# One exponential and one logarithm for the first image's preparation, the last halves' routing after the last weights, and roots by GpSimd's power

## The chip, the cores and the metric

The kernel runs on one core of a Trainium2 chip. The metric is device time in microseconds, the median of several executions. The core has five engines with instruction queues of their own: TensorE (PE) for matmuls, VectorE (DVE), ScalarE (ACT), GpSimd (POOL) and SyncE (SP), which issues transfers here. An engine takes its instructions in order, so one that waits holds up all those behind it.

## The reference

The input `x` is 4 images of 256 channels and 32 x 32 places, so 1024 tokens an image. Two layers follow one another; cut to what matters:

```python
# layer 0
x = x + proj(attention(ln_c(x)) + pe)         # 8 heads, softmax over the dyn_k highest scores of a row
t = tokens(x)
t = t + moe0(ln_t(t))                         # 8 experts, the best 2, 256 -> 256 -> 256, exact GELU; moe0(u) = u + experts
x = image(t)
# layer 1
u = ln_c(x)
delta = softplus(u @ W_delta + b_delta)
Bm, Cm = u @ W_B, u @ W_C
h[l] = exp(delta[l] * -exp(A_log)) * h[l-1] + delta[l] * u[l] * Bm[l]     # 16 states
y = sum over states of h * Cm, + u * D        # in four orders of the places, and their mean
x = x + y
t = tokens(x)
t = t + moe1(ln_t(t))                         # 8 experts, the best 2, 256 -> 1024 -> 256
```

`ln_c` and `ln_t` subtract the mean over channels and divide by the root of the variance plus 1e-6 or 1e-5.

## The kernel before, in words

**Stages.** Norms and projections run to about 110 us, the attention to about 1960, the layer-0 expert tiles to about 2196, the scans of layer 1 to about 3432, and the layer-1 expert tiles to the end.

**Attention** is an order of 64 half-head turns (8 heads, 2 halves, 4 images), each of which finds the threshold of 128-row groups by counting and then masks, exponentiates and sums. `turn(i)` writes out the order by hand. At five places in a turn (`PLACES`) it calls `beside`, which takes a step from other work: `plan(first, needed, steps)` puts a generator on the list `todo`, with the place from which it may run and the turn at which it is due, and `beside` takes the one that is due earliest. A generator that yields True goes on at the next call before others do. The last turns carry three of these: `doubts()`, which checks that all thresholds were found (`all_sure` L977 and L978, matmul `tot` L980, `bad` L982), and `last_image(0)` and `last_image(1)`, which route the two halves of the last image.

**Routing of a half** is `halved`. PE multiplies the tokens by the router (`raw`, L356) and transposes them into PSUM (`tp`, called `turned` in the profile, L361). ACT copies each 128 tokens into the rows to be sent (L366) and squares them in place with a sum along the row (L367), which gives the variance. DVE finds the two best experts (L371 to L382), PE counts how many tokens each expert has (`counted`, L225 to L230), DVE takes the root of the variance by a bit trick and three Newton steps (L387 to L393), ACT forms one exponential (L394), and DVE works out places and weights (L398 to L412). POOL then sends the rows to their experts' slots in memory (`send`, L214), and `table` makes the list of tiles.

In these last turns the attention itself ends: PE forms scores (L878) and adds the mask (L883), ACT exponentiates (L891), PE sums with the values (L901), DVE divides (L910, L911), PE projects (L713) and DVE adds the residual (L716).

**Layer-0 expert tiles.** `Tile0` has 256 rows of one expert. SP loads rows and weights, DVE and ACT normalise (`xn`, L1449 and L1451), PE transposes (L1458), DVE copies (`xe`, L1460), PE multiplies (`hp`, L1483), ACT applies GELU (`hid`, L1485), PE multiplies again (`yp`, L1491), DVE adds the bias (`ys`, L1494), ACT and DVE scale and add the residual (L1498, L1500) and POOL stores (L1502). There are 36 such tiles. After each tile the loop takes up to six steps from each generator in a list `beside`: among them, from the tile FIRST − 1 on, gathering image 0's results (`whole(0)`, L1882), its preparation for the scans and then `lead`, and from SECOND − 1 on `whole(1)`. The order of the instructions of this stage within an engine is chosen by the framework's scheduler from priorities, not by hand.

**Preparation**, `Prep.steps`, is a generator too. For one image: mean and difference `xm`, squares `ln_sq`, variance `ln_ve`, its root by the bit trick and three Newton steps on DVE (L1794 to L1798), multiplication (`ln_rb`), the 32 rows of B and C (`bp`, L1815 to L1818, stored to memory as `bc_d`), then four parts `zp` of the projection (L1837). Softplus is built as max(z, 0) + ln(1 + exp(−|z|)): relu (L1841), absolute value (L1842), exponential (L1843), what adding 1 loses of the exponential (`lost`, two DVE operations), logarithm (L1847), and then sums and products (L1851 to L1856). `whole_rows` is False for the first image, whose preparation runs beside the tiles, and True for the others, which are prepared during the scans. Where `whole_rows` is True the parts at the end are whole rows of 1024. In the tile stage `xm` and `ln_sq` share a tag with two buffers, and `bc` and `v` share the buffer `sp`.

**Lead** is the start of the first scan: `lead_cum` (L1920) on DVE, `lead_uu` (L1922) on POOL and a copy of it on ACT.

**Scans.** There are 4 x 2 x 16 turns of one image, one half of the channels and one state, in an order written by hand. In a turn DVE runs the forward scan `forth` (L2055), the backward scan `back` (L2062, into PSUM), the product `yc` (L2089), the short scan `come` over rows (L2068), then a step of the other generators, preparation and routing, and then the column scan `h` (L2079). ACT forms decays (L2022, L2026, L2030) and a column copy of the inputs (L2039); POOL forms `gap` (L2059), the inputs `uu` (L2038) and `da_c` (L2073); PE adds all directions into one sum (L2044, L2050, L2084) and the outputs over the states (L2093).

Of the kernel before, what the change touches and what calls it, by code (L numbers as in the profile page):

```python
# [14 lines left out]
I32 = mybir.dt.int32  # L15
I8 = mybir.dt.int8
AF = mybir.ActivationFunctionType
ALU = mybir.AluOpType
# [5 lines left out]
C = 256  # L24
# [3 lines left out]
NT = L // P  # L28
# [34 lines left out]
def metaformer(ctx: ExitStack, tc: tile.TileContext, t: dict, out: bass.AP):  # L63
    nc = tc.nc
# [279 lines left out]
    def halved(b, h, space, bank, wide_bank):  # L344
# [17 lines left out]
        yield True  # L362
        nc.vector.tensor_scalar(nm, raw[:, :, E], -C ** -0.5, None, ALU.mult)
        nc.vector.tensor_copy(lg, raw[:, :, :E])
        for i in range(M):
            nc.scalar.copy(xr[b][:, M * h + i, :C], tp[:, i])  # L366
            nc.scalar.activation(tp[:, i], tp[:, i], AF.Square, bias=nm[:, i : i + 1], scale=C ** -0.5,  # L367
                                 accum_out=ve[:, i : i + 1])

        def best(value, hot):  # L370
            nc.vector.tensor_reduce(value, lg, AX.X, ALU.max)  # L371
# [98 lines left out]
    with ExitStack() as st:  # L470
# [454 lines left out]
        def plan(first, needed, steps, places=range(PLACES)):  # L925
            todo.append([first, needed, steps, False, places])
# [48 lines left out]
        def doubts():  # L975
            sure = p2.tile([P, 1], F32, tag="fr", name="all_sure", bufs=1)
            nc.vector.tensor_reduce(sure, fine, AX.XY, ALU.add)  # L977
            nc.vector.tensor_scalar(sure, sure, 2.0 * (2 * B * NT) * 4 - 0.5, None, ALU.is_ge)  # L978
            tot = bank("tot")[:, 0:1]
            nc.tensor.matmul(tot, mean_w, sure, start=True, stop=True)  # L980
            yield True
            nc.vector.tensor_scalar(bad, tot[0:1], (P - 0.5) / C, None, ALU.is_lt)  # L982
            yield False

        plan(70 * PLACES, 100.5, doubts())

        def last_image(h):
            while not images[B - 1].ready[h]:
                yield None
            yield from halved(B - 1, h, scratch("space1"), bank, lambda: wide_ps("turned"))  # L990
            if h == NHALF - 1:
                yield from table(scratch("space2"), bank)

        for h in range(NHALF):
            plan((68 + 2 * h) * PLACES, 100 + h, last_image(h))

        def beside(i, place=None):

# [759 lines left out]
    class Prep:  # L1758
# [7 lines left out]
        def steps(self, room, psum, tag, whole_rows):  # L1766
# [4 lines left out]
            for h in range(NHALF):  # L1771
# [6 lines left out]
                    nc.vector.tensor_tensor(xm[:, c, cols], x[b][:, c, cols], mean, ALU.subtract)  # L1778
                    nc.scalar.activation(sq[:, c, cols], xm[:, c, cols], AF.Square)
                yield  # L1780
            ve, r0, rr, rs = (room(f"ln_{i}", [NT]) for i in ("ve", "r0", "rr", "rs"))
            for h in range(NHALF):
                var = psum.tile([P, HALF], F32, tag=tag, name="ln_var")[:, : NT // NHALF]
                for i in range(NT // NHALF):
# [6 lines left out]
                if h == 0:  # L1791
                    yield
            yield
            nc.vector.tensor_scalar(r0.bitcast(I32), ve.bitcast(I32), -0.5, RSQRT_BITS, ALU.mult, ALU.add)  # L1794
            for src, dst in ((r0, rs), (rs, r0), (r0, rs)):
                nc.vector.tensor_tensor(rr, src, src, ALU.mult)
                nc.vector.scalar_tensor_tensor(rr, rr, -0.5, ve, ALU.mult, ALU.mult)
                nc.vector.scalar_tensor_tensor(dst, rr, 1.5, src, ALU.add, ALU.mult)  # L1798
            yield
            yield  # L1800
            for h in range(NHALF):
# [27 lines left out]
            def lost(c, cols):  # L1829
                back = self.dx[:, c, cols]  # L1830
                nc.vector.tensor_scalar(back, v[:, c, cols], 1.0, 1.0, ALU.add, ALU.subtract)
                nc.vector.tensor_tensor(back, v[:, c, cols], back, ALU.subtract)

            for i, (c, cols) in enumerate(parts):
                zp = psum.tile([P, HALF], F32, tag=tag, name="zp")
                for k in range(CT):
                    nc.tensor.matmul(zp, wd[:, k, ts(c, P)], xm[:, k, cols], start=(k == 0), stop=(k == CT - 1))  # L1837
                if i:
                    lost(*parts[i - 1])
                yield  # L1840
                nc.scalar.activation(self.delta[:, c, cols], zp, AF.Relu, bias=bd[:, c : c + 1])  # L1841
                nc.scalar.activation(v[:, c, cols], zp, AF.Abs, bias=bd[:, c : c + 1])  # L1842
                nc.scalar.activation(v[:, c, cols], v[:, c, cols], AF.Exp, scale=-1.0)  # L1843
                yield
            lost(*parts[-1])
            yield
            nc.scalar.activation(v, v, AF.Ln, bias=1.0)  # L1847
            yield
            for c, cols in [(c, slice(0, L)) for c in range(CT)] if whole_rows else parts:
                dx = self.dx[:, c, cols]  # L1850
                nc.vector.tensor_tensor(dx, dx, v[:, c, cols], ALU.add)  # L1851
                nc.vector.tensor_tensor(self.delta[:, c, cols], self.delta[:, c, cols], dx, ALU.add)
                yield
                yield
                nc.vector.tensor_tensor(dx, self.delta[:, c, cols], xm[:, c, cols], ALU.mult)
                nc.vector.scalar_tensor_tensor(x[b][:, c, cols], xm[:, c, cols], dsk[:, c : c + 1],  # L1856
                                               x[b][:, c, cols], ALU.mult, ALU.add)
                yield
                yield
# [69 lines left out]
    with ExitStack() as st:  # L1929
# [4 lines left out]
        def room(name, shape):  # L1934

            tag = "d" if name in ("xm", "ln_sq") else name
            return pb.tile([P, *shape], F32, tag=tag, name=name, bufs=1 if name == "sp" else None)
# [477 lines left out]
```

## Time and profile before

| | us |
|---|---|
| median of three executions | 3968.95 (3959.26, 3968.95, 3977.5) |
| the profiled execution, its span | 3982.76, 3979.8 |
| PE busy | 3387.3 (85%) |
| DVE busy | 3024.2 (76%) |
| ACT busy | 2799.2 (70%) |
| POOL busy | 1934.2 (49%) |
| granted PE clock, whole span | 0.875 |

By stage, from the same execution:

| stretch, us | PE busy | DVE busy | ACT busy | POOL busy | granted PE clock |
|---|---|---|---|---|---|
| 110 to 1960, attention | 1463.85 | 1609.88 | 1635.08 | 1032.32 | 0.78 |
| 1960 to 2196, layer-0 tiles | 190.16 | 161.25 | 112.58 | 91.95 | 0.90 |
| 2196 to 3432, scans | 1132.06 | 1133.68 | 875.48 | 712.47 | 0.97 |
| 3432 to 3960, layer-1 tiles | 498.47 | 78.16 | 141.23 | 90.46 | 0.98 |

A line of a timeline gives the start and the duration in microseconds, the engine, the source line, the operation, the tile written and the tiles read with their shapes, and how many neighbouring instructions are merged in it. Brackets give the engine's idle time just before and what ended it. Busy time is a sum over an engine's instructions; an idle engine costs nothing unless another waits for it.

### The profile page before, as it was taken

How to read it: one execution, taken by the hardware profiler on the slowest of the kernel's cores; microseconds unless marked ns; L12 is line 12 of the kernel's file. 1: busy time of each engine (PE TensorE's matmuls, PEld its weight loads, DVE VectorE, ACT ScalarE, POOL GpSimd, SP SyncE). 2: the span in 40 equal slices, each digit the busy share in tenths (PEclk: the TensorE clock that was granted, in tenths of full speed). 3: DMA queues.
4: the chain of work that ended last, by engine and by line, in shares of the span. 5: the costliest groups of instructions: out<-in, count | busy, mean ns of one | idle time of the engine just before them, and what ended most of it. 6: DMA issues, size and time to landing. Idle time of an engine off the chain costs nothing. (4 is left out here: it accounts for less than half of the span.)

```text
span 3979.8 us, 49680 instructions
## 1 busy us (share of the span) xinstructions
PE 3387.3 (85%) x17330; PEld 1898.6 (48%) x17330; DVE 3024.2 (76%) x5204; ACT 2799.2 (70%) x3748; POOL 1934.2 (49%) x1671
## 2 busy tenths in 40 slices
PE   8477888888888888886597889988988989999996
PEld 5133443534354444543375333443433433788885
DVE  3589898998989898989476899999999999201112
ACT  2889999899989999996245677767767767322222
POOL 0145544585648574685343667555555556221111
PEclk8578887788778787788798999999999999999997
DMA  9400075000000000000284444334324333655555
GB/s 295 106 1 1 1 221 134 1 1 25 17 1 1 1 33 1 1 11 17 95 243 129 130 122 138 116 111 125 125 100 131 123 116 128 214 187 184 187 194 187
DMA packets 241814, 393.71 MB, mean 99 GB/s; under 512 B 31888, under 2 KB 182160, under 8 KB 241424
## 3 DMA queue, kind: packets, MB, share of 16 engines
q1 hardware_dynamic: 218016, 340.54, 27.5%
q0 software_dynamic: 19904, 48.48, 3.8%
q8 instruction: 139, 2.28, 0.2%
q10 hardware_dynamic: 3632, 1.40, 0.1%
q14 instruction: 123, 1.01, 0.1%
HBM read 280.41 MB, written 109.94 MB: 98 GB/s over the span
## 5 line engine op out<-in xcount | busy, mean ns | idle before, releaser
L823 POOL TENSOR_SCALAR dr<-s_n,last 128x1024 bf16<-128x1024 f32 x250 | 719.4, 2893 | 734.3 <-DVE state L851 396.8
L733 ACT ACTIVATE junk_a<-s_n,state 128x1024 int8<-128x1024 f32 x448 | 514.7, 1149 | 25.3 <-DVE state L857 9.0
L2073 POOL TENSOR_TENSOR da_c<-prod,come 128x1024 f32<-128x1024 f32 x128 | 256.6, 2005 | 389.3 <-DVE h L2079 333.7
L737 DVE TENSOR_SCALAR_CACHE_REDUCE junk_v<-s_n,state 128x1024 int8<-128x1024 f32 x320 | 408.7, 1277 | 8.8
L2263 ACT ACTIVATE hid<-hp,b 128x256 f32<-128x256 f32 x288 | 134.1, 474 | 361.6 <-PE hp L2261 361.3
L784 DVE SCALAR_TENSOR_TENSOR w<-s_n,win 128x1024 f32<-128x1024 f32 x256 | 350.9, 1371 | 5.3
L787 DVE MAX8 win<-w 128x8 f32<-128x1024 f32 x256 | 314.5, 1228 | 8.8
L2084 PE MATMUL sum<-h,ident 128*128 128x512 f32 x512 | 261.4, 635 | 61.3 <-DVE h L2079 59.1
L2062 DVE TENSOR_TENSOR_SCAN sum<-da,uu 128x1024 f32<-128x1024 f32 x127 | 289.9, 2282 | 29.7 <-PE sum L2044 22.2
L891 ACT ACTIVATE ex<-sT 128x1024 f32<-128x1024 f32 x256 | 247.0, 1016 | 88.6 <-PE sT L883 88.5
L2038 POOL TENSOR_TENSOR uu<-dx,bb 128x1024 f32<-128x1024 f32 x127 | 308.3, 2428 | 1.6 <-DMA bb<-bc_d 1.6
L733 ACT ACTIVATE junk_a<-s_n,guess 128x1024 int8<-128x1024 f32 x256 | 294.3, 1150 | 7.2
L2055 DVE TENSOR_TENSOR_SCAN h<-da,uu 128x1024 f32<-128x1024 f32 x127 | 288.4, 2271 | 1.1 <-POOL uu L2038 1.1
L2079 DVE TENSOR_TENSOR_SCAN h<-da_c,uu 128x1024 f32<-128x1024 f32 x127 | 288.8, 2274 | 0.0
L901 PE MATMUL o_ps<-ex,vT 128*32 128x256 f32 x2048 | 238.0, 448 | 57.0 <-ACT ex L891 43.6
L2050 PE MATMUL sum<-da_c,ident 128*128 128x512 f32 x512 | 255.8, 623 | 26.0 <-POOL da_c L2073 22.4
L2272 DVE TENSOR_TENSOR ys<-yp,b2e 128x512 f32<-128x512 f32 x36 | 24.9, 691 | 326.3 <-PE yp L2269 326.3
L2022 ACT ACTIVATE da_c<-delta,a_log 128x1024 f32<-128x1024 f32 x128 | 268.4, 2097 | 5.2 <-DMA rows_y<-ys 5.2
L2261 PE MATMUL hp<-xe,w 128*128 128x256 f32 x1152 | 259.2, 383 | 9.4 <-DVE xe L2249 5.9
L2274 POOL DMA_INDIRECT results<-ys,to x72 | 69.3, 962 | 407.3 <-DVE ys L2272 200.3
L2050 PE MATMUL sum<-h,twice 128*128 128x512 f32 x512 | 248.0, 607 | 12.0 <-DVE sum L2062 12.0
L767 ACT COPY s_n<-sp 128x1024 f32<-128x1024 f32 x256 | 245.4, 1003 | 18.1 <-PE sp L759 10.3
(676 smaller groups left out, 7557.4 us busy)
## 6 DMA issues: line engine op xcount, KB each, us to landing
cb<-bc_d SPq DMA_DIRECT2D x128, 512.0 KB, 4.1
bb<-bc_d SPq DMA_DIRECT2D x127, 512.0 KB, 5.0
w<-in_w SPq DMA_DIRECT2D x36, 1024.0 KB, 5.3
w2e<-in_w SPq DMA_DIRECT2D x36, 1024.0 KB, 5.5
slots_x<-zeros SPq DMA_DIRECT2D x1, 33669.0 KB
slots_x<-zeros SPq DMA_DIRECT2D x1, 33282.0 KB
w<-in_w SPq DMA_DIRECT2D x72, 256.0 KB, 3.1
xs<-slots_x SPq DMA_DIRECT2D x36, 261.0 KB, 3.3
```

The costliest lines, as they stand in the source:

```text
L733: nc.scalar.activation(junk, self.row(r), AF.Sign, bias=thr, scale=-1.0, accum_out=u)
L737: nc.vector.tensor_scalar(junk, self.row(r), thr, None, ALU.is_lt, ALU.add, accum_out=u)
L784: nc.vector.scalar_tensor_tensor(w, self.row(r), self.win[:, r, 0:1], self.row(r), ALU.is_gt if r < LAST_DVE else ALU.is_ge, ALU.subtract, ...
L787: nc.vector.max(out=self.win[:, r, 1:], in_=w)
L823: ins = eng.tensor_scalar(dr, self.row(r), self.last[:, r : r + 1], None, ALU.is_lt)
L2022: nc.scalar.activation(grid(self.da_c), cols_flipped(self.prep.delta[:, self.c]), AF.Exp, scale=self.decay)
L2038: nc.gpsimd.tensor_tensor(self.uu[:, 0], self.prep.dx[:, self.c], self.bb, ALU.mult)
L2050: nc.tensor.matmul(self.sum[:, ts(h, HALF)], ident if eye is None else eye, view[:, ts(h, HW // NHALF), :], start=False, stop=last)
L2055: nc.vector.tensor_tensor_scan(rows.rearrange("p r w -> p (r w)"), self.da, self.uu[:, 0], 0.0, ALU.mult, ALU.add)
L2062: nc.vector.tensor_tensor_scan(self.sum[:, ::-1], self.da[:, ::-1], self.uu[:, 0][:, ::-1], 0.0, ALU.mult, ALU.add)
L2079: nc.vector.tensor_tensor_scan(self.hs, self.da_c, self.uu[:, 1], 0.0, ALU.mult, ALU.add)
L2084: nc.tensor.matmul(cols_flipped(self.sum[:, ts(h, HALF)]), ident, grid(self.hs)[:, :, ts(h, half)], start=False, stop=False)
```

## The change

Three things are edited. In `halved`, the squares go to a scratch row and come before the copies. In the plans, `doubts()` comes two turns' worth of places earlier, and the first half's routing three places later. In `Prep.steps`, the root is one operation of GpSimd, for all images; and where `whole_rows` is False, the four exponentials are one over all four parts, followed at once by the logarithm into the buffer `sq`, with the `lost` operations after that.

```diff
@@ halved
+        junk = room([C])
+        for i in range(M):
+            nc.scalar.activation(junk, tp[:, i], AF.Square, bias=nm[:, i : i + 1], scale=C ** -0.5,
+                                 accum_out=ve[:, i : i + 1])
         for i in range(M):
             nc.scalar.copy(xr[b][:, M * h + i, :C], tp[:, i])
-            nc.scalar.activation(tp[:, i], tp[:, i], AF.Square, bias=nm[:, i : i + 1], scale=C ** -0.5,
-                                 accum_out=ve[:, i : i + 1])
@@ the plans
-        plan(70 * PLACES, 100.5, doubts())
+        plan(68 * PLACES, 99.5, doubts())
...
         for h in range(NHALF):
-            plan((68 + 2 * h) * PLACES, 100 + h, last_image(h))
+            plan((68 + 2 * h) * PLACES + 3 * (1 - h), 100 + h, last_image(h))
@@ Prep.steps
-            ve, r0, rr, rs = (room(f"ln_{i}", [NT]) for i in ("ve", "r0", "rr", "rs"))
+            ve, rs = room("ln_ve", [NT]), room("ln_rs", [NT])
...
-            nc.vector.tensor_scalar(r0.bitcast(I32), ve.bitcast(I32), -0.5, RSQRT_BITS, ALU.mult, ALU.add)
-            for src, dst in ((r0, rs), (rs, r0), (r0, rs)):
-                nc.vector.tensor_tensor(rr, src, src, ALU.mult)
-                nc.vector.scalar_tensor_tensor(rr, rr, -0.5, ve, ALU.mult, ALU.mult)
-                nc.vector.scalar_tensor_tensor(dst, rr, 1.5, src, ALU.add, ALU.mult)
+            nc.gpsimd.tensor_tensor(rs, ve, minus_half, ALU.pow)
...
-                if i:
+                if i and whole_rows:
                     lost(*parts[i - 1])
                 yield
                 nc.scalar.activation(self.delta[:, c, cols], zp, AF.Relu, bias=bd[:, c : c + 1])
                 nc.scalar.activation(v[:, c, cols], zp, AF.Abs, bias=bd[:, c : c + 1])
-                nc.scalar.activation(v[:, c, cols], v[:, c, cols], AF.Exp, scale=-1.0)
+                if whole_rows:
+                    nc.scalar.activation(v[:, c, cols], v[:, c, cols], AF.Exp, scale=-1.0)
                 yield
-            lost(*parts[-1])
-            yield
-            nc.scalar.activation(v, v, AF.Ln, bias=1.0)
-            yield
+            log = v if whole_rows else sq
+            if whole_rows:
+                lost(*parts[-1])
+                yield
+                nc.scalar.activation(log, v, AF.Ln, bias=1.0)
+                yield
+            else:
+                nc.scalar.activation(v, v, AF.Exp, scale=-1.0)
+                nc.scalar.activation(log, v, AF.Ln, bias=1.0)
+                yield
+                for part in parts:
+                    lost(*part)
+                    yield
...
-                nc.vector.tensor_tensor(dx, dx, v[:, c, cols], ALU.add)
+                nc.vector.tensor_tensor(dx, dx, log[:, c, cols], ALU.add)
```

`minus_half` is a column of −0.5 that the kernel had already. `lost` is unchanged: dx = v − ((v + 1) − 1).

## The prediction

> **What bounds the kernel.** I read the page first, then the busy time cut by stage, then the timelines of the three places that the diff touches.
>
> ```profile
> PE 3387.3 (85%) x17330; PEld 1898.6 (48%) x17330; DVE 3024.2 (76%) x5204; ACT 2799.2 (70%) x3748; POOL 1934.2 (49%) x1671
> ...
> PE 12%; DMA 1%; issue 1%; POOL 0%; DVE 0%; ACT 0%; DVEq 0%; POOLq 0%; SPq 0%
> ```
>
> The whole span is bound by no one engine, so each edit must be priced in its own stage. The chain that ended last follows only the last stage: all but a few shares are the matmuls of the layer-1 expert tiles, which the change leaves alone.
>
> The second view is busy time by stretch inside the layer-0 expert tiles. Columns are PE, PEld, DVE, ACT, POOL, the granted clock, the DMA share and GB/s.
>
> ```profile
> 1976.00:2080.00 104.00, 95.13 (x449) 76.92 (x447) 77.62 (x270) 46.70 (x97) 51.11 (x60) 0.97 0.80 236
> ...
> 2112.00:2157.00 45.00, 30.72 (x104) 21.15 (x103) 27.09 (x66) 33.34 (x44) 14.49 (x10) 0.83 0.46 126
> ```
>
> In the quiet stretch PE works 95 of 104 us at a clock of 0.97: those tiles are PE's. In 2112 to 2157, where the first image is prepared for the scans, PE works 31 of 45 us at 0.83 and ACT is the busiest. ACT's timeline there (start, duration, line, operation; idle before it in brackets) says why.
>
> ```profile
> 2126.97 1.28 ACT L1843 ACT_TABLE_LOAD   x1
> 2128.27 0.63 ACT L1843 ACTIVATE sp<-sp 128x512 f32<-128x512 f32 x1
> 2128.91 1.28 ACT L1485 ACT_TABLE_LOAD   x1
> 2130.21 0.47 ACT L1485 ACTIVATE hid<-hp,b1e 128x256 f32<-128x256 f32 x1
> ...
> 2136.94 1.28 ACT L1847 ACT_TABLE_LOAD   x1
> 2138.23 1.91 ACT L1847 ACTIVATE sp<-sp 128x2048 f32<-128x2048 f32 x1
> ```
>
> Every exponential of the preparation (L1843) lies between two GELUs (L1485), each with a table load of 1.28 us ahead of it. From 2116.2 to 2144.1 I count ten loads: four before L1843, five before L1485, one before L1847. From 2113.9 to 2144.1 ACT idles some 0.5 us. Results L1494 end tiles at 2109.74, 2122.10, 2132.79, 2138.57, 2155.87 and 2162.43: five tiles in 52.7 us, where quiet tiles come every 4.34 us.
>
> At the end of attention, ACT and PE:
>
> ```profile
> 1922.43 0.20 ACT L367 ACTIVATION_READ_ACCUMULATOR turned<-turned,space 128x1 f32 x1
> 1925.04 0.20 ACT L394 ACTIVATE space<-space 128x4 f32<-128x4 f32 x1 [2.40 <-DVE space L393]
> 1925.15 1.92 ACT L891 ACTIVATE ex<-sT 128x1024 f32<-128x1024 f32 x2
> ```
>
> ```profile
> 1926.21 1.56 PE L901 MATMUL o_ps<-ex,vT 128*32 128x256 f32 x6 [2.94 <-ACT ex L891]
> ...
> 1937.98 0.35 PE L980 MATMUL tot<-all_sure,mean_w 128*128 128x1 f32 x2 [1.16 <-DVE all_sure L978]
> 1938.57 1.95 PE L356 MATMUL raw<-rw,x 128*128 128x9 f32 x16 [0.24 <-DVE bad L982]
> ```
>
> The last two exponentials are queued behind the halved routing: L394 waits 2.40 us for the roots on DVE. So PE's last weighted sums start at 1926.21 after 2.94 us of idleness, and cold: they take 4.4 us (1926.21 to 1930.6), while the same work took 1.95 us at 1914.40. The second half's router then waits for a check (tot L980, bad L982) that has nothing to do with it.
>
> In a scan turn:
>
> ```profile
> 2920.60 0.21 DVE L2068 TENSOR_TENSOR_SCAN come<-prod,gap 128x32 f32<-128x32 f32 x1
> ...
> 2920.73 0.15 DVE L1794 TENSOR_SCALAR ln_r<-ln_ve 128x8 int32<-128x8 int32 x1
> ...
> 2922.52 0.17 DVE L1798 SCALAR_TENSOR_TENSOR ln_rs<-ln_rr,ln_r 128x8 f32<-128x8 f32 x1
> 2922.60 2.28 DVE L2079 TENSOR_TENSOR_SCAN h<-da_c,uu 128x1024 f32<-128x1024 f32 x1
> ...
> 2925.03 1.91 POOL L2073 TENSOR_TENSOR da_c<-prod,come 128x1024 f32<-128x1024 f32 x1 [7.02 <-DVE h L2079]
> ```
>
> ```profile
> 2576.96 1.68 POOL L1712 TENSOR_TENSOR nm_s<-nm_ve,minus_half 128x8 f32<-128x8 f32 x1
> ...
> 2577.53 0.21 DVE L2068 TENSOR_TENSOR_SCAN come<-prod,gap 128x32 f32<-128x32 f32 x1
> ...
> 2588.08 3.64 POOL L1718 TENSOR_TENSOR nm_s<-nm_ve,minus_half 128x8 f32<-128x8 f32 x1
> ```
>
> Ten small DVE operations (L1794 to L1798) sit between the short scan of L2068 and the column scan L2079. PE's L2084, POOL's L2073 and the next turn wait for L2079.
>
> [...]the exponential starts 1.30 us after the load does (2126.97, 2128.27). I price a load at 1.283 us. [...]The trace has a load before L1847, but with GELUs between; the program after the change still issues one load for the exponential and another for the logarithm, so I count three loads. [...]the power of L1712 took 1.68 us, and L1718, started inside a column scan, 3.64.[...]
>
> **Part 1, the last halves.** Removed: tot and bad from before the second half's router, L394 from before the exponentials. Moved: doubts and the last weights ahead of half 0, whose 4 copies now follow its 4 squares. Walk after: tot at about 1916.3, weights to 1918.9, raw and turned (2.8 us in the old trace) to 1921.7, sums straight behind them and warm, to 1923.6. The four squares, at 0.46+0.20 us less overlap, 0.61 to 0.66 each, end near 1924.1 (the copy-and-square pairs took 0.875 each, 3.5 in all[...]). DVE's chain L387 to L412 takes 4.57 us (1922.67 to 1927.24), now to 1928.7. The reciprocal of the weighted sums (L910) is behind it on DVE, so it starts at 1928.7, not 1930.65: −2.0. From there to the end of L716 is 6.9 us as before: 1935.5; the second router starts there, not at 1938.57: −3.1. The squares of half 1 then save another 1.0: L387 at 1941.6 against 1945.70, −4.1. The copies add 4 x 0.28 us behind them, hidden by DVE's chain, and the sends come later. The counting matmuls end near 1944.0, just when L398 wants them. The sends (eight of 1.265 us on POOL), the table and the first tile's load follow: **−4.0 us**, between −2 (if L398 waits) and −5.
>
> **Part 2, the preparation beside the tiles.** Removed: seven of ten loads, 7 x 1.283 = 9.0 us, and four exponentials of 0.63 for one as long as the logarithm on the same shape (1.91): −0.6. Added: one buffer, no transfer. ACT is what limits the stretch, so PE's idleness there (2.02+1.85+1.69+3.13+1.98 us ahead of single rows, more in small ones) and cold matmuls (four of L1483 in 2.05 us where warm ones take 1.06) should mostly go. Walked tile by tile, ends are 2102.3, 2108.6, 2115.2, 2124.2, 2134.8, 2138, 2146 where before had 2102.59, 2109.74, 2122.10, 2132.79, 2138.57, 2155.87, 2162.43: −16 us. In exchange, the two loads, exponential, logarithm and GELU load stand in one block: 3 x 1.28 + 2 x 1.91 plus two result operations of 1.0, 8.7 us, in which a GELU waits and PE idles 5 to 7 us; that is inside the walk. The twelve DVE adds of 0.69 us each (L1851 to L1855), lead_cum (2.28) and lead_uu (4.46 on POOL, with ACT's copy waiting 3.8 and hid behind it 3.61) come three steps later (26 steps become 29), into tiles that had been quiet: +3. **−13 us**, bounds −17 (nothing given back) and −6 (the block costs PE its full 8.7 and its matmuls are cold after it).
>
> **Part 3, roots by GpSimd.** Removed from DVE, for four images: ten operations of 0.15 to 0.17, 1.87 us from 2920.73 to 2922.60. Added on POOL: one power, 1.68, behind uu (L2038) and ahead of da_c (L2073), before which POOL idles 5 to 7 us: hidden[...]. At 2576.96 a power ran across L2068 and did not delay it. Three images lie in the scans: 3 x 1.87 = 5.6 if all comes off the turn; ACT's copy of uu (L2039) ends at the instant at which L2079 starts, but belongs to the next turn. I take 4.5, for a delay of the short scan in the turns where uu ends just before it (bounds 0 and −5.6). In the tile stage, before the gathers, I count 0: PE waits there for the gathers and the interleaved tile.
>
> **Sum.** −4.0 −13 −4.5 = −21.5 us. The profiled execution took 3982.76 us (span 3979.8), 13.8 above the median of 3968.95, whose three runs spread over 18. The sum against its own time gives 3961.3; the saving carries over to the median: 3947.5, so **3947**.
>
> **Rivals.** *A, forecast*: the three add, 3938 to 3957. *B, the merged block becomes the stall*: PE waits its full 8.7 us and lead_uu moves into a quiet tile; part 2 gives 5, parts 1 and 3 give 6: −11, 3958. For it: the program puts both loads between two GELUs, and nothing there covers PE. Against: today's ten loads already stall five tiles. *C, tile stage fully healed*: five tiles at 4.4 plus the preparation's own 6 us of PE work, 28 against 52.7: −24, with the rest −32, 3937. Against: DVE and POOL work stays. *D, slower*: the layer-1 tiles have PE busy 498 of 528 us at a clock of 0.98; that stretch decides if the clock falls. To end 0.5% slower in spite of −21.5 it must lose 41 us: 0.98 x 528/569 = 0.91 or lower. At 0.90 it lasts 575 us, +47, the sum +25: 3994. Attention runs at 0.78[...]. *E, no root gain[...]*: 0 for part 3[...]: 3951.
>
> **How the numbers follow.** A 0.60, B and E 0.22, C 0.11, D 0.07. 0.5% is 19.8 us, about what a measurement of this kernel can tell from no change: faster means below 3949.1. A's middle lies 2 us below that, so 0.38 of its 0.60; with C 0.49, and 0.03 of E's edge: faster 0.52. D, its milder forms counted as within: slower 0.06. The rest, 0.42, is the same. The range that leaves out 2 in 10 is 3931 to 3964; the likeliest alone 3938 to 3957.
>
> **What would show it.** Three table loads in the tile stage, two of them next to each other but for results; the five tiles in about 37 us; a granted clock there above 0.9; no idleness of PE before the last sums and their length near 2 us; the sends starting near 1947; turns with the power as short as their neighbours. I am wrong if PE idles over 7 us at the logarithm, if the power delays L2068, or if tiles after 2160 lose what the five won.

## The result and the profile after

The kernel after takes 3959.6 us (median of 11 executions, 3951.34 to 3965.8) against 3973.98 us for the kernel before (11 executions, 3959.26 to 3984.95): a ratio of 0.9963 with a 95% interval of 0.9948 to 0.9978. That is 14.4 us, and the interval reaches from 9 to 21. The forecast was a gain of 21.5 us to 3947, with "faster by over 0.5%" the likeliest outcome; the measured gain is 0.37%. The median of the kernel before had been 3968.95 when the forecast was made and is 5 us higher with more executions, so the gain was missed by 7 us and the total by 12.6. The profiled execution took 3952.81 us, its span 3951.0.

The two profiled executions differ by more, 28.8 us of span, and half of that is not the change's. I compare them at places where the same work starts. "The reference sums" are PE's weighted sums of the attention's last pair but one (L901 before, L903 after), which lie ahead of everything that was edited.

| from ... to ... | before, us | after, us | difference |
|---|---|---|---|
| start of the execution, the reference sums | 1914.40 | 1900.12 | −14.3 |
| the reference sums, the second half's first send | 36.63 | 35.12 | −1.5 |
| that send, the last tile's result (L1494, L1496) | 244.12 | 239.47 | −4.7 |
| that result, the first forward scan | 0.88 | 0.88 | 0 |
| the first forward scan, the 128th (L2055, L2063) | 1178.04 | 1169.88 | −8.2 |
| the 128th, the end | 605.7 | 605.5 | −0.2 |

The first row is the same program in both kernels and varies by itself: in the 13 traces of this study the reference sums start between 1898.7 and 1914.4. The other rows add up to 14.5 us, close to the 14.4 of the medians. So these stages brought 1.5, 4.7 and 8.2 us, where the forecast had 4, 13 and 4.5 for the parts that it placed in them. From here on "the boundary", "the tile stage" and "the scans" are rows two, three and five.

The page of the kernel after, its busy line and the chain that ended last:

```profile
PE 3373.9 (85%) x17330; PEld 1889.9 (48%) x17330; DVE 3017.3 (76%) x5164; ACT 2789.5 (71%) x3738; POOL 1936.6 (49%) x1675
...
PE 12%; DMA 1%; issue 1%; POOL 0%; DVE 0%; ACT 0%; DVEq 0%; POOLq 0%; SPq 0%
```

Nothing moved there: the end is still the layer-1 tiles. Busy time by stretch, columns as before (the quiet stretch, and that of the preparation, both 15 us earlier than in the kernel before):

```profile
1961.00:2065.00 104.00, 95.13 (x447) 76.78 (x445) 76.95 (x266) 46.40 (x98) 51.01 (x61) 0.97 0.82 237
2097.00:2142.00 45.00, 32.68 (x119) 23.25 (x118) 31.14 (x79) 25.17 (x37) 15.56 (x13) 0.81 0.55 155
```

The quiet tiles are the same to a hundredth. The stretch of the preparation has ACT at 25 us, not 33, but PE works only two microseconds more, and its clock is 0.81, where over 0.9 was forecast.

ACT in that stretch. The ten table loads are three:

```profile
2109.75 1.28 ACT L1851 ACT_TABLE_LOAD   x1
2111.05 1.91 ACT L1851 ACTIVATE sp<-sp 128x2048 f32<-128x2048 f32 x1
...
2113.96 1.28 ACT L1852 ACT_TABLE_LOAD   x1
2115.25 1.91 ACT L1852 ACTIVATE ln_sq<-sp 128x2048 f32<-128x2048 f32 x1
2117.18 1.28 ACT L1487 ACT_TABLE_LOAD   x1
```

They are where the prediction's walk put them: an exponential, two result operations and a logarithm stand between the loads, 8.7 us in one piece. But PE, in the same stretch, waits longer than the walk said, and the longest wait is not for ACT:

```profile
2119.00 2.08 PE L1485 MATMUL hp<-xe,w 128*128 128x256 f32 x4 [4.22 <-ACT hid L1487]
...
2134.25 2.08 PE L1485 MATMUL hp<-xe,w 128*128 128x256 f32 x4 [6.42 <-DVE xe L1462]
```

After the 4.22 us for the GELU come 6.42 us for a copy of a transposed tile (xe, L1462) on DVE. DVE, from a few microseconds earlier (lines of its timeline, many small ones left out):

```profile
2126.48 2.31 DVE L1474 TENSOR_TENSOR wt<-best,xs 128x2 f32<-128x2 f32 x1
...
2131.13 0.68 DVE L1909 COPY x<-op 128x512 f32<-128x512 f32 x1
...
2133.52 0.67 DVE L1462 COPY xe<-tp 128x512 f32<-128x512 f32 x1
```

From 2125.3 to 2139.8 DVE has no idle time. It has a 128x2 operation that takes 2.31 us while lead_uu runs on POOL (2126.22 to 2128.77; the same operation takes 0.14 us at 2134.12), the additions, a copy of image 1 (L1909) and tile results, and the xe that PE wants stands behind them.

At the boundary, ACT, PE and DVE (below, PE is called warm when its granted clock is full, 1.00, and cold when it is half, 0.50):

```profile
1904.09 1.94 ACT L893 ACTIVATE ex<-sT 128x1024 f32<-128x1024 f32 x2 [4.09 <-PE sT L885]
...
1911.91 0.20 ACT L396 ACTIVATE space<-space 128x4 f32<-128x4 f32 x1 [1.32 <-DVE space L395]
```

```profile
1907.04 0.64 PE L903 MATMUL o_ps<-ex,vT 128*32 128x256 f32 x8
...
1912.20 2.05 PE L715 MATMUL pp<-att,wproj 128*128 128x512 f32 x2 [0.97 <-DVE space L405]
1916.28 2.08 PE L715 MATMUL pp<-att,wproj 128*128 128x512 f32 x2 [2.03 <-DVE att L913]
1919.14 3.56 PE L715 MATMUL pp<-att,wproj 128*128 128x512 f32 x4 [0.78 <-DVE x L718]
1923.49 1.95 PE L356 MATMUL raw<-rw,x 128*128 128x9 f32 x16 [0.79 <-DVE x L718]
```

```profile
1914.02 1.75 DVE L912 RECIPROCAL rden<-o_ps 128x256 f32<-128x256 f32 x1
```

The order is as forecast: exponentials ahead of the squares, sums at 1907.04 warm and with no wait, the division at 1914.02, 13.9 us after the reference sums where it had been 16.25. But then the projection: two, two and four matmuls in 2.05, 2.08 and 3.56 us. In the kernel before they had taken 1.13, 1.12 and 1.98:

```profile
1930.53 1.13 PE L713 MATMUL pp<-att,wproj 128*128 128x512 f32 x2
1932.92 1.12 PE L713 MATMUL pp<-att,wproj 128*128 128x512 f32 x2 [1.27 <-DVE att L911]
1934.83 1.98 PE L713 MATMUL pp<-att,wproj 128*128 128x512 f32 x4 [0.78 <-DVE x L716]
```

The clock over the projection, after and before (busy times by stretch, the granted clock behind POOL's), is half and full:

```profile
1912.20:1922.30 10.10, 7.29 (x8) 2.15 (x8) 4.37 (x16) 0.00 (x0) 5.79 (x6) 0.50 0.18 66
```

```profile
1930.40:1940.50 10.10, 6.65 (x29) 3.50 (x28) 3.96 (x7) 0.00 (x0) 5.76 (x6) 1.00 0.26 93
```

In the scans, a turn with a root:

```profile
2893.75 1.64 POOL L1796 TENSOR_TENSOR ln_rs<-ln_ve,minus_half 128x8 f32<-128x8 f32 x1
...
2894.73 0.21 DVE L2076 TENSOR_TENSOR_SCAN come<-prod,gap 128x32 f32<-128x32 f32 x1
...
2894.85 2.26 DVE L2087 TENSOR_TENSOR_SCAN h<-da_c,uu 128x1024 f32<-128x1024 f32 x1
...
2897.26 1.91 POOL L2081 TENSOR_TENSOR da_c<-prod,come 128x1024 f32<-128x1024 f32 x1 [1.87 <-DVE h L2087]
```

The power runs on POOL across L2076 (come) without delaying it, and the column scan L2087 starts right behind. The turn that took 12.02 us takes 8.42.

### The profile page after: what moved, and what is told of

Same layout as the page of the kernel before. It is cut to its first block, busy times and chain, and to the rows that moved or that the text cites. A ratio compares the mean times of both kernels' runs of the same rounds, so it can differ in the third digit from the quotient of the medians.

```text
span 3951.0 us, 49637 instructions
## 1 busy us (share of the span) xinstructions
PE 3373.9 (85%) x17330; PEld 1889.9 (48%) x17330; DVE 3017.3 (76%) x5164; ACT 2789.5 (71%) x3738; POOL 1936.6 (49%) x1675
## 3 DMA queue, kind: packets, MB, share of 16 engines
q8 instruction: 139, 2.28, 0.2%
## 5 line engine op out<-in xcount | busy, mean ns | idle before, releaser
L2063 DVE TENSOR_TENSOR_SCAN h<-da,uu 128x1024 f32<-128x1024 f32 x127 | 288.1, 2269 | 1.0 <-POOL uu L2046 1.0
L2087 DVE TENSOR_TENSOR_SCAN h<-da_c,uu 128x1024 f32<-128x1024 f32 x127 | 288.5, 2272 | 0.0
L903 PE MATMUL o_ps<-ex,vT 128*32 128x256 f32 x2048 | 236.2, 450 | 50.1 <-ACT ex L893 35.7
L2277 PE MATMUL yp<-w2e,hid 128*128 128x256 f32 x1152 | 255.6, 380 | 0.0
```

Source lines behind the costliest of these rows:

```text
L2063: nc.vector.tensor_tensor_scan(rows.rearrange("p r w -> p (r w)"), self.da, self.uu[:, 0], 0.0, ALU.mult, ALU.add)
L2087: nc.vector.tensor_tensor_scan(self.hs, self.da_c, self.uu[:, 1], 0.0, ALU.mult, ALU.add)
L2277: nc.tensor.matmul(yp[:, a], self.hid[:, f, ts(a, P)], self.w2[:, f, :], start=(f == 0), stop=(f == NF - 1))
```

## The experiments

All times of segments are from traces, with the places named above. Totals are given where they were timed.

### Each part alone

The kernel before, with one part of the diff at a time.

Part 1, `halved` and the plans:

> The kernel before with the edit of the last halves and their plans alone. Two traces gave: from the start of the last weighted sums but one to the first send of the second half 36.6 us before and 35.1 after. Theory (the edit won its 2 us at the division of the last sums and lost them again, because the projection behind it now runs on a cold clock): 35.1 again, the eight projection matmuls of the last half 7 to 8 us of PE time where the kernel before took 4.2. Rival (the small gain is chance of one trace, the forecast of 4 us holds): 32.5 with projections as before. Total: 1 to 2 us under the kernel before, or 4; neither can be told by the median alone. Tile stage from the result 14 tiles before the last to the last: 115.7 as before.

Measured: ratio 1.000 (0.9985 to 1.0015). Boundary 35.54 us, and the projection is cold again:

```profile
1910.77 2.04 PE L715 MATMUL pp<-att,wproj 128*128 128x512 f32 x2 [0.96 <-DVE space L405]
1914.85 2.07 PE L715 MATMUL pp<-att,wproj 128*128 128x512 f32 x2 [2.04 <-DVE att L913]
1917.70 3.56 PE L715 MATMUL pp<-att,wproj 128*128 128x512 f32 x4 [0.78 <-DVE x L718]
```

The theory's figures hold: 35.5 us at the send, and 7.7 us for the eight projection matmuls. From the reference sums to the last tile's result the two traces agree within 0.01 us (280.74, before 280.75): the first 22 tiles took 2.1 us longer than in the kernel before, the last 14 one less, in the same order of instructions. Part 1 alone is worth nothing that can be seen.

Part 2, the merged exponential and logarithm:

> The kernel before with the merged exponential and logarithm of the first image alone; the roots stay on DVE. From the result 14 tiles before the last to the last tile's result: 115.7 us before, 110.5 after the whole change. Theory (the merge alone gives 5 and the root of image 0 nothing): 110 to 111, with PE idle some 4 us for the GELU behind the logarithm and some 6 us for a transposed tile's copy behind the additions of the preparation. Rival (the root moved to GpSimd held the gathers up and cost part of the merge's gain): 107 or less. The three root turns of the scans as before: 9.7, 10.3, 10.3 to 12.0.

Measured: ratio 0.9973 (0.9960 to 0.9985), some 11 us. 14 tiles to the last took 100.81 us, 14.9 less than before, and the whole tile stage 231.35, 12.8 less. The theory (110 to 111) falls, and the rival's figure (107 or less) holds; its cause, the gathers held up, is tested below. The merge alone gives the sum that was forecast for it, and more than the whole change gives in this stage. Behind the merged block tile results (L1494, from 2127.44 on) come 11.9, 2.8, 6.1 and 6.0 us apart. PE's two longest waits there:

```profile
2131.79 2.07 PE L1483 MATMUL hp<-xe,w 128*128 128x256 f32 x4 [3.57 <-ACT hid L1485]
...
2140.02 1.99 PE L1491 MATMUL yp<-w,hid 128*128 128x256 f32 x8 [1.32 <-DVE ys L1494]
```

The wait for the GELU behind the logarithm is there, 3.57 us; the 6.42 us for xe are not. DVE is even fuller than in the kernel after (37 of the 45 us from 2112 to 2157, 34 there after), with a 128x2 operation of 2.30 us beside lead_uu in it too. But in this order no copy xe stands on DVE between 2123.7 and 2141.1, and PE does not need one: its matmuls at 2131.79 and 2137.15 read tiles copied before.

Part 3, the roots by GpSimd:

> The kernel before with the roots by GpSimd alone. Distance of the forward scans over the turn of the root: 9.71, 10.31, 12.02 us before; 7.82, 10.05, 8.42 after. Theory (each root gives its full 1.87, and the rest of the 8.1 us that the scans differ is matmuls that ran at half clock in one turn or another by chance): each of the three turns near 7.8 to 8.4 unless a sum of column matmuls in it takes 2.9 to 3.6 us instead of 2.0, which adds 1.6; scans in all shorter by 5.6 give or take 3. Rival (the power also removes something in other turns): the turns 48 to 49 and 80 to 81, counted from the first, 1.7 shorter again. Tile stage: 115.7, give or take 0.5.

Measured: ratio 0.9967 (0.9953 to 0.9980), some 13 us. The root turns took 7.82, 10.05 and 8.43, the scans 1171.56, as the theory said. But the rival's sign came too: the turns 48 and 80 took 8.62 us each, 1.7 less than before. In both, four matmuls ahead of the turn ran cold before and warm here. Those of turn 48 in the kernel before, at a granted clock of 0.54:

```profile
2650.49 3.68 PE L2050 MATMUL sum<-h,twice 128*128 128x512 f32 x4 [2.72 <-DVE sum L2062]
```

With the roots on POOL the four take 1.98 us. So these turns are shorter by the cause that the theory names, PE's clock, though hardly by chance (in nine of ten traces for turn 48, see below). What nobody expected is that the tile stage too, which has one root of 1.87 us in it and PE waiting for other things, took 236.48 us, 7.6 less than before. So in the tile stage the merge alone is worth 12.8 us, the root alone 7.6, and both together 4.7 (one trace each).

### What is wrong with the tiles after

First, whether the loads hold them up. This kernel leaves the first image's exponential and logarithm out and keeps two operations of their shape.

```diff
-                nc.scalar.activation(v, v, AF.Exp, scale=-1.0)
-                nc.scalar.activation(log, v, AF.Ln, bias=1.0)
+                nc.scalar.activation(v, v, AF.Identity, scale=0.1)
+                nc.scalar.activation(log, v, AF.Identity, scale=0.5)
```

> The kernel after with the first image's exponential and logarithm replaced by a scaled copy of the same shape, so that softplus is left out there and no table is loaded in the tile stage. 14 tiles to the last: 110.5 with the three loads. Theory A (the block of three loads and two long operations stalls the GELU and cools PE's clock, which is where the missing gain is): 104 to 106. Theory B (the additions, the copies of image 1[...] on DVE are what limits the tiles after the block): 109 or more, since they stay.

Measured: 107.43, between the two. No load is left, and PE still waits:

```profile
2124.12 1.15 PE L1485 MATMUL hp<-xe,w 128*128 128x256 f32 x4 [2.56 <-ACT hid L1487]
...
2132.42 2.08 PE L1485 MATMUL hp<-xe,w 128*128 128x256 f32 x4 [3.71 <-DVE xe L1462]
...
2138.49 1.86 PE L1485 MATMUL hp<-xe,w 128*128 128x256 f32 x4 [3.14 <-ACT hid L1487]
```

The wait for the GELU shrank from 4.22 to 2.56 us; the one for xe is still there, 3.71, with another for a GELU behind lead_uu's copy. The framework also put instructions into a somewhat other order, so that the 3.1 us are not the loads' price alone. What it shows is that the three loads are not where all of the missing 8 us went.

Then the root of image 0 on DVE again, all else as after:

```diff
-            nc.gpsimd.tensor_tensor(rs, ve, minus_half, ALU.pow)
+            if whole_rows:
+                nc.gpsimd.tensor_tensor(rs, ve, minus_half, ALU.pow)
+            else:
+                # the bit trick and three Newton steps of the kernel before
```

> The kernel after, but the root of image 0, beside the tiles, is formed by the bit trick on DVE again; the other three roots stay on GpSimd. 14 tiles to the last: 115.7 us in the kernel before, 110.5 after, 100.8 with the merge alone, 108.2 with the roots alone. Theory (the two edits disturb each other in the tile stage only, through the place of image 0's root, and add up elsewhere): 100 to 102 in the tile stage, the root turns of the scans 7.8, 10.1 and 8.4 as after; in all some 9 us below the kernel after, near 0.994 of the kernel before. Rival (the merge alone got its 14.9 us from one lucky execution): 108 or more again, and a total like that of the kernel after.

Measured: 102.89 us for the 14 tiles, the whole tile stage 233.81 (−10.3), root turns 7.82, 10.05, 8.43, scans 1171.63. Ratio to the kernel before 0.9954 (0.9935 to 0.9973). The theory holds in the tile stage: the order on all engines there is that of part 2 alone, and the time comes with it. It fails in the total, which is 0.1% (some 4 us) under the kernel after, where 9 us were expected, and these intervals don't tell the two apart. The trace shows where the gain went. From the reference sums to the end it takes 2052.2 us, the kernel after 2050.9: 5.7 us less in the tile stage, but 0.7 more at the boundary, 1.8 in the scans, and 4.6 from the 128th forward scan to the end. There, where the first layer-1 tile is begun, PE runs cold for a while. The same stretch, from 20 to 31 us behind that scan, here and in the kernel after:

```profile
3376.04:3387.04 11.00, 9.73 (x40) 7.40 (x41) 3.23 (x7) 3.06 (x8) 0.00 (x0) 0.70 0.98 326
```

```profile
3365.47:3376.47 11.00, 10.48 (x61) 8.74 (x60) 2.72 (x6) 5.88 (x17) 0.00 (x0) 1.00 1.02 333
```

This is not one trace's accident alone. From the 128th scan to the end, the traces of part 3 alone, of this kernel and of the last two runs below took 609.6 to 610.1 us, and that of the next one 613.0, all with such a cold stretch; part 2 alone took 607.3, with a shorter one, and the other seven 605.3 to 606.2. What decides it is not shown.

Is it the power as such, on POOL's queue ahead of the gathers, or the order that the framework makes of it? The same kernel with the power added, into a buffer that nobody reads:

```diff
             else:
+                nc.gpsimd.tensor_tensor(room("ln_unread", [NT]), ve, minus_half, ALU.pow)
                 # the bit trick and three Newton steps
```

(Three small buffers had one copy and not two, to make room.)

> As the run before this one, but GpSimd forms image 0's root too, into a buffer that nobody reads, at its place ahead of the gathers; the order of instructions on PE, DVE and ACT is that of the run before this one. Theory A (the tile stage loses because the power waits on POOL's queue for the variance and holds the gathers of image 1 up): 14 tiles to the last 107 or more. Theory B (it loses because the framework, reckoning with another time for the root, puts the instructions of PE and DVE into another order): 100 to 103.

Measured: 101.53 us, with the power in its place ahead of the gathers:

```profile
2090.81 1.68 POOL L1799 TENSOR_TENSOR ln_unread<-ln_ve,minus_half 128x8 f32<-128x8 f32 x1 [4.14 <-DVE wt L1474]
2092.68 1.09 POOL L1898 DMA_INDIRECT y<-rows_y,slot  x1 [0.19 <-PE hp L1485]
```

Theory B holds and A falls. POOL waits 4.14 us for DVE, takes 1.68 us for the power, the gathers start after it, and the tiles do not mind. With the same order of instructions on PE, DVE and ACT the tile stage is that of the merge alone. Nobody waits for the power's result here; in the kernel after PE does, but only for 0.3 us (`ln_rb`, 2081.32). And traces of one order agree, whatever else is different in their kernels: 115.7 and 114.7 us for 14 tiles in that of the kernel before, 110.5 and 111.1 in that of the kernel after, 100.8 to 102.9 in four of part 2's. What costs 8 us is the other order in which the framework lays out tiles and preparation when the root is GpSimd's. That the framework reckons with another time for the root, as theory B says, is an assumption: no run shows its reasons.

Which work in that order is in the way? Two empty tiles ahead of the lead:

```diff
-chain(whole(0), preps[0].steps(room, ps_n, "t", False), lead.steps(preps[0]))
+chain(whole(0), preps[0].steps(room, ps_n, "t", False), pause(12), lead.steps(preps[0]))
```

> The kernel after with twelve empty steps, two tiles, ahead of the lead of the first scan, so that lead_uu on GpSimd and its copy on ACT come later, and lead_cum on DVE with them. 14 tiles to the last: 110.5. Theory ([...]the scan of lead_cum fall into the tiles where DVE is full, and that is where 5 us or more go): 105 or less. Rival (DVE is full there from the additions and the copies of image 1 alone, and an order that holds the copy of the next tile back): 109 to 112, with PE idle some 6 us again ahead of one tile's first matmuls.

Measured: 107.17 us. The same two waits of PE, to the hundredth:

```profile
2135.47 2.07 PE L1485 MATMUL hp<-xe,w 128*128 128x256 f32 x4 [4.22 <-ACT hid L1487]
...
2151.13 2.07 PE L1485 MATMUL hp<-xe,w 128*128 128x256 f32 x4 [6.41 <-DVE xe L1462]
```

The run does not test what it was made for: POOL's order came out unchanged, lead_uu stands where it stood and a 128x2 operation on DVE takes 2.30 us beside it; only lead_cum and ACT's copy moved. The 3.3 us less come later, in the two tiles that they left (10.78 and 6.02 us for 12.01 and 9.01). The wait for xe did not move, so lead_cum and ACT's copy are not its cause, as the rival said, though its total was too high. What the long operation beside lead_uu costs stays open.

And the additions spread over more tiles:

```diff
                 yield
                 yield
+                yield from pause(0 if whole_rows else 2)
```

(after each of the two pairs of operations of a part)

> The kernel after with two empty steps more after each addition of the first image's preparation, so that the last four parts reach over five tiles and not three. 14 tiles to the last: 110.5. Theory (DVE is what limits the three tiles after the logarithm): 106 or less. Rival (the work only moves to later tiles and the sum stays): 109 to 112.

Measured: 103.72 us, 6.8 less. PE waits for the GELU as before, and no longer for xe:

```profile
2127.48 2.08 PE L1485 MATMUL hp<-xe,w 128*128 128x256 f32 x4 [4.22 <-ACT hid L1487]
...
2138.58 1.13 PE L1485 MATMUL hp<-xe,w 128*128 128x256 f32 x4 [1.21 <-ACT hid L1487]
```

So the 6.42 us are DVE's: additions, image 1's copies and the tiles' own work in one stretch, with the next tile's xe behind them. Spread, they fit. (The spread changed the order of other instructions too, so how much of it the additions alone are is not separated.)

### The boundary

Six matmuls of constants in PE's wait, after the first half's counting:

```diff
         counted(sums, both, M)
+        warm()      # b = 3, h = 0 only: six matmuls ident x 256 columns of wproj into a spare bank
```

> The kernel after with six matmuls of constants, into a bank that nobody reads, behind the first half's counting matmuls, where PE waits 5 us for the division on DVE. From the start of the last weighted sums but one to the first send of the second half: 36.6 us in the kernel before, 35.1 to 35.8 in five traces with the edit. Theory (the division comes 2 us earlier, but the projection behind it runs on a clock that has gone cold in PE's wait, and gives 2.5 us back): 32.5 to 33.5, with the last four projection matmuls near 2.0 us instead of 3.56. Rival (the projection is slow for another cause, its operands or PSUM's banks): 35 to 36, projections as slow.

Measured: 33.95 us at the send, a little outside what the theory said:

```profile
1917.85 4.48 PE L997 MATMUL warm<-wproj,ident 128*128 128x256 f32 x12
1922.13 2.03 PE L716 MATMUL pp<-att,wproj 128*128 128x512 f32 x4
1924.94 1.98 PE L716 MATMUL pp<-att,wproj 128*128 128x512 f32 x4 [0.78 <-DVE x L719]
1927.71 2.34 PE L356 MATMUL raw<-rw,x 128*128 128x9 f32 x16 [0.78 <-DVE x L719]
```

The last four projection matmuls take 1.98 us, not 3.56, and the second router starts 20.8 us after the reference sums, not 23.4. That is 3.3 us earlier than in the kernel before, where 3.1 were forecast. The cause is shown: it is the clock, not the operands or the banks. The granted clock is 1.00 from 1922.3 to 1929.1, over these matmuls, and 0.50 over the constants from 1918.9 to 1922.2. One microsecond is lost again before the sends, since the second half's own router and transposes now ran slower (2.34 and 1.95 for 1.95 and 1.51). In this trace nothing was left of it by the last tile (278.3 from the reference sums, 274.6 after): the first 22 tiles took 4 us longer than in the kernel after. Two traces of the same tile order differ that much, so a microsecond or two at the boundary can't be followed to the end.

The division and projection ahead of both halves' routing, with image 0's root on DVE:

```diff
-            plan((i + 21) * PLACES + 1, i + 23, images[b].finish(1), (1, 3))
+            plan((i + 21) * PLACES + 1, i + 23, images[b].finish(1), (1, 3) if b + 1 < B else range(PLACES))
...
-            plan((68 + 2 * h) * PLACES + 3 * (1 - h), 100 + h, last_image(h))
+            plan((69 + h) * PLACES + 1 - h, 100 + h, last_image(h))
```

> The kernel after with image 0's root on DVE, and the last half's division and projection ahead of both halves' routing (the first half's routing begins one turn later, and the projection may use every place). From the start of the last weighted sums but one to the last of the sixteen sends' start: 44.0 us in the kernel after. Theory (the division waits behind the first half's chain on DVE for 5 us, and that is what the order can still give): 38 to 41, the sends now one behind the other on POOL, 1.27 us each. Rival (the first half's routing, coming later, holds the second half's up, and the sum stays): 43 to 45. Tile stage 101 to 103.

Measured: 50.3 us from the reference sums to the last send, 6.3 more than after. The division did come early, but the first half's router did not start until the projection's last addition was done:

```profile
1915.88 3.68 PE L715 MATMUL pp<-att,wproj 128*128 128x512 f32 x4 [0.78 <-DVE x L718]
1920.34 1.95 PE L356 MATMUL raw<-rw,x 128*128 128x9 f32 x16 [0.78 <-DVE x L718]
```

and both halves' chains on DVE came behind it, one after the other, with PE cold for much of it (the second half's router took 3.55 us, where it takes 1.95 warm). Rival and theory were both too low; the first half's routing is worth more early, where it hides behind the last weights. The tile stage was 101.59 us for 14 tiles; ratio to the kernel before 0.9958 (0.9943 to 0.9973).

The same with the spread of the additions:

> As the run before this one, and with the additions of the first image's preparation spread by two empty steps each. 14 tiles to the last: 101 to 103 with image 0's root on DVE, 103.7 with the spread and the root on GpSimd. Theory (the spread helps only where DVE was overfull, and with the other order it is less so): 99 to 103. In all: the scans' 8.6, the tile stage's 13 and the last halves' 4 us together, 3948 to 3954, about 0.993 to 0.994 of the kernel before, faster than the kernel after by 0.2 to 0.3%. Rival (they do not add): as the kernel after, 0.996.

Measured: 104.36 us for 14 tiles and 0.9956 (0.9939 to 0.9974). With image 0's root on DVE the spread helps nothing, it costs a little; the two cures are for the same trouble. The forecast for the total, 3948 to 3954, did not come either: it was 3964.2, and the rival, that they do not add, fits. No version of these is told apart from the kernel after by its total. The one with the root of image 0 on DVE has the lowest ratio; from the reference sums to the end the trace with the additions spread is the shortest (2048.3 us).

## Why the prediction was right and where it was not

**Sign and range: right.** 3959.6 lies in 3931 to 3964, and the three mechanisms exist: ten loads became three, the exponentials left the routing's queue, the roots left the turn. The likeliest outcome, a gain over 0.5%, did not come. Part of the fit is luck: part 3 brought 3.7 us more than forecast, most of it by PE's clock, and this covers part of what parts 1 and 2 lacked.

**Part 1, forecast −4.0 (−2 to −5); measured −1.5 at the send, 0 at the end of the tiles.** The step that failed is "from there to the end of L716 is 6.9 us as before". It took 9.4: 1914.02 to 1923.43. In the kernel before PE was cold during the sums, from 1923.49 to 1930.3, and warm again for the projection; in the kernel after PE does the sums early and warm, then 32- to 8-column counting, then waits 0.97 us for DVE, and the projection pays: the clock is 0.50 from 1912.12 to 1922.36. So the cold stretch was moved, not removed: the prediction took the sums for warm and the projection for unchanged. The 2.35 us won at the division (forecast 2.0) went there, as the run with the constants shows. Also small: L398's wait for the counting, put at nothing, was 0.53 us.

**Part 2, forecast −13 (−6 to −17); measured −4.7 for the stage in the whole change, −12.8 alone.** The sizes of loads and the block were right, and the merge alone gives the forecast's sum, though not by its terms. The five tiles that were to shrink from 52.7 to about 37 us took 42.3 with the merge alone, 10.4 less and not 16, and the tiles around them gained 4.5 us where 3 were to be given back; that these errors cancel is luck. In the kernel after the five took 47.7 us. For the whole change, the step that failed is the root: "In the tile stage, before the gathers, I count 0". It is not 0 in this stage, where the order is the framework's: the runs with the roots alone, with image 0's root on DVE and with the unread power show that changing the engine of an operation of 1.7 us moves 8 us here, in either direction, and that it is the order that moves them, not the operation. The give-back that I took for 3 us (additions, lead_cum and lead_uu in later tiles) shows as one wait of PE of 6.4 us in the order of the kernel after; with the additions spread it is gone.

**Part 3, forecast −4.5 (0 to −5.6); measured −8.2 for the scans in this pair, −8.8 as the mean of ten traces with the power over three without.** The turn with the first root lost 1.89 us in every trace, and the delay of the short scan that I took off 5.6 for did not come. The third turn lost 3.6, of which 1.6 are four matmuls that ran cold there in all three traces without the power; in the second, 1.6 of the 1.87 went the other way. A further 1.7 us fell off the turn 48 in nine of ten traces and off the turn 80 in four, by four matmuls of 3.68 us that became warm. So the term was undersized by matmuls at half clock, which I had not counted as something that a scan turn could lose or win.

**Rivals.** B's total of 3958 is closest, but not by its mechanism: the merged block stalls PE 4.22 us in the kernel after and 3.57 in the merge alone, whose stage is 8 us shorter. C did not come, D neither: from the 128th forward scan to the end both kernels took 605.6 us. E fell: three loads are there, and the roots gain. Of the signs that were to show an error, none came: PE idled 4.22 us at the logarithm, not over 7, the power did not delay the short scan, and the tiles behind the five took 32.8 us, as before.

## What to carry to other kernels

Where a scheduler orders the instructions, cost an edit there by the new order, not by the operation: an edit of 2 us moved the stage by 8, and edits that gain alone need not add; each should be tried alone. Where an order is written by hand, as in the scans, the removed time came off to 0.02 us in one turn of three; in the other two a change of PE's clock took 1.6 us of it away or added as much. A stage's gain should be followed to the end of the kernel: in one trace here 5.7 us won in the tile stage were lost again, most of them at a colder start of the layer-1 tiles (a granted clock of 0.70 against 1.00 over 11 us). And work that an engine does earlier can leave a later step worse off: here PE did its sums earlier and warm, and the projection behind them met a clock of 0.50 and took 7.7 us where it had taken 4.2.

## What the runs showed of the hardware

The loss of PE's clock comes and goes at the same places in several traces. PE on the column sums of the turn with the third root, before and after, at a granted clock of 0.53 and 1.00:

```profile
2913.12 3.59 PE L2084 MATMUL sum<-h,ident 128*128 128x512 f32 x4 [0.21 <-DVE ln_ve L1790]
```

```profile
2888.94 1.99 PE L2092 MATMUL sum<-h,ident 128*128 128x512 f32 x4 [0.58 <-DVE ln_ve L1792]
```

and of the turn with the second root, after, at 0.66:

```profile
2587.01 2.88 PE L2092 MATMUL sum<-h,ident 128*128 128x512 f32 x4 [0.66 <-DVE ln_ve L1792]
```

Four such matmuls take 1.98 us where the clock is full. They took 3.5 to 3.6 at the first place in all three traces without the power; with it, 1.98 or 1.99 in six of ten, and 3.6 in the other four. At the second place the slow case (2.5 to 3.2) came in all ten traces with the power and in one of three without. What decides between two traces of one order is not shown; the waits ahead of the matmuls shown were 0.2 to 0.7 us. In the trace of the kernel after the clock is only ever full or half, and each of the 102 stretches at half lasts a multiple of 3.41 us, within 0.15 us (in that of the kernel before 107 of 108 do).

At the boundary the clock was lost behind a stretch of work. In the kernel before it is full up to 1923.49 and half from there on, though PE was busy for 3.06 of the 3.41 us ahead of that point:

```profile
1920.08:1923.49 3.41, 3.06 (x36) 2.75 (x32) 1.71 (x12) 2.50 (x9) 0.00 (x0) 1.00 0.02 5
1923.50:1930.30 6.80, 4.09 (x32) 1.55 (x32) 3.18 (x23) 2.03 (x3) 1.95 (x2) 0.50 0.05 20
```

The counting matmuls of 8 to 32 columns are 1.9 us of that stretch (1921.35 to 1923.28). In the run with six matmuls of constants the clock fell at 1918.88, behind the same counting and one microsecond into the constants, with PE busy for 3.07 of 3.41 us. What made it fall in these two traces is not shown. Of the 2.94 us of idleness ahead of the cold sums, from 1923.28 to 1926.21, all but 0.21 us lie behind the fall, and so are not its cause.

A power of 128x8 on GpSimd took 1.63 to 1.69 us for every root in the traces, and its run across the short scan L2076 (0.21 us) delayed neither of the two. In the kernel before, the power L1718 began 0.12 us behind the start of a column scan of 2.28 us and took 3.64 us. The power L1712 (2576.96 to 2578.64) was still running when the next column scan began at 2577.66, and that scan took its usual 2.27 us.
